# A recurrent attention layer with a sign-weight feed-forward gate: one load of the sums of squares, an earlier weight request, and two steps moved at a change of block

## The chip, the cores and the metric

The kernel runs on one core of a Trainium2 chip. A core has a matrix engine (TensorE, PE in the profile, with PEld for its weight loads), a vector engine (VectorE, DVE), a scalar engine (ScalarE, ACT), GpSimd (POOL) and SyncE (SP). SP issues most of the transfers between the large memory and the on-chip memory, and POOL issues those that add to what is already there. The matrix engine writes its results into result banks (PSUM), of which this kernel keeps six for its projections, and ScalarE or VectorE has to empty a bank before it can be used again.

The metric is device time in microseconds (us) for one execution; less is better.

## What is computed

The input x has 2048 tokens of 512 numbers. After a layer norm over the 512 numbers, the attention part runs 16 heads of 128 channels (2048 channels in all), and a feed-forward part of 2048 hidden units makes a gate. Inputs and outputs are float32. Cut to what matters:

```
xn = layernorm(x)
q, k, v = conv(silu(xn @ Wq)), conv(silu(xn @ Wk)), conv(silu(xn @ Wv))   # causal, 4 taps per channel
q, k = rotate(q), rotate(k);  q, k = q / |q|, k / |k|                      # per head and token
out = sum over s in 0..3 of  (q . lag(k, s)) / sqrt(128) * sigmoid(lag(a, s) * b) * lag(v, s)
out = out * rsqrt(mean(out^2) + eps) * norm_w * z                          # mean over all 2048 channels
s   = out @ Wout
g   = silu(relu(xn @ sign(up) * up_scale) @ sign(down) * down_scale * output_scale)
result = x + s * g
```

(The gate z is silu(xn @ Wz); a and b are xn @ Wa and xn @ Wb, one number per head and token.) The dots q . lag(k, s) need only four lags, so no token looks further back than three. The mean of out^2 needs all channels of a token. The kernel leaves this factor out of the output projection and applies it at the very end, when s is combined with g; for that it collects the sums of out^2, called o's sums below.

## The kernel before

**Tiling.** Channels lie on the 128 partitions and tokens along them. The tokens are cut into 4 blocks of 512 (index b), the heads into 8 pairs (index p, 256 channels each). The unit of work is `step(p, b)` (line 557). It makes q and k of pair p for block b + 1 and multiplies them (`queries`, `products`), and in the same step it makes v, the weighted sum o, the gate z and, every second pair, the output projection for pair p of block b. So attention runs one block behind the dots. The steps of block -1 (line 675) make only q and k, with the first quarter of the feed-forward part between them. Blocks 0 to 2 follow (line 695). A last stage (lines 699 to 761) does v, o, z and the projections of block 3, and a closing part (line 763 on) does the feed-forward part for blocks 1 to 3 and combines all.

**What happens when a block changes.** In the step with p = 0 and b >= 0 (`change` in line 560), all of block b's dots and squares of q and k are known, and the weights of v are made from them:

- `sum_squares` (line 390) adds the squares of q and k over channels, on TensorE; `sum_dots` (line 401) does so with the products for one pair or two.
- `norms(b)` (line 425) takes these squares through a copy and a square root on ScalarE and an addition and a maximum on VectorE.
- `norms_in_rows(b)` (line 438) takes the reciprocal on VectorE and then sends it to the rows rk and rq with eight transfers on SP.
- `coefficients(b)` (line 452) multiplies the rows with the gates and the dots in three VectorE instructions and writes the coefficients to memory (`co_dram`). `weighted` (line 483) later loads them back, spread over the channels, as bc ("coefficient rows"), in four transfers per pair; bc has three buffers.

For b = 1 and 2 the norms stand between q's and k's work (lines 564 to 568). For b = 0, and only there, they follow `products` (lines 569 to 571).

**Output projections** are collected in `outputs_due` and run by `output_projections` (line 550). One of them (line 528) covers two pairs and runs over four chunks of 128 tokens. After the last pair of a block `sums_of_o` (line 409) follows: TensorE adds o's squares over channels, POOL writes two rows of 512 sums into `ss_dram`, the second adding to the first, and SP loads them into `ss_acc`, one number per token with tokens on partitions (line 418).

**The order of work.** TensorE and VectorE execute in the order of the source: every instruction of theirs is pinned behind the one before it (`InOrder`, line 68; all show as line 76 in the profile). The instructions of ScalarE, SP and POOL are ordered by a planner. It issues what its own model of time takes as ready, the earlier in the source first, so a request for weights can be issued long ahead of its place in the source when its buffer is free. Within each engine's queue the order is then fixed. Buffers are shared by tag: the weights of v and z share three (`load`, line 246), rk and others share one.

**The last stage.** For block 3, line 700 on requests the weights of v for pairs 0 and 1, and the loop at line 730 requests those of pair p + 1 in round p, for p from 1 to 6. POOL loads the feed-forward part's signs for the up product in that loop (line 748). At its end line 759 takes a square root of all of `ss_acc` on ScalarE into `rms`, and VectorE the reciprocal. In the closing part POOL loads the signs for the down product (line 768), and hidden units go through `hid` (ScalarE, line 627), two casts on VectorE (`hid_hi`, `hid_lo`) and the down products.

Of the kernel before, what the change touches and what calls it, by code (L numbers as in the profile page):

```python
# [44 lines left out]
P = 128  # L45
# [8 lines left out]
NP = H // 2  # L54
TB = 512
NTB = S // TB
TC = TB // P
# [24 lines left out]
def recurrent_layer(ctx: ExitStack, tc: tile.TileContext, a: dict, out: bass.AP):  # L82
    nc = tc.nc
# [215 lines left out]
    outputs_due = []  # L299
# [24 lines left out]
    def products(p, b, q, between=None, beside_k=None):  # L324

        n = f"_{p}_{b}"
        load(qks, "k", p, b)
        q0 = q[:, LAGS - 1]
        k = with_halo(qks, "k", "k", 1, p, b)
        raw = raw_of(qks, "k", p, b)  # L330
        if p % 2 == 0:
            sum_squares()
        convolve(1, p, raw, k[:, :, HALO:])
        keep_halo("k", k, p, b)
        if between:
            between()
        turn(q)
        if beside_k:
            beside_k()

        sq = [qks.tile([P, 2, TB], F32, tag=f"sq{j}", name=f"sq{j}" + n, bufs=2 - j) for j in range(2)]
        for j in range(2):
            nc.scalar.activation(sq[j][:, 0], q0[:, j], AF.Square)
            nc.scalar.activation(sq[j][:, 1], k[:, j, HALO:], AF.Square)
        nc.gpsimd.dma_start(sq[0], sq[1], accum_op=ALU.add)
        squares_due.append((p, sq[0]))
        def product(to, j, lo, hi):

            k0 = k[:, j, lo : lo + TB]
            k_lags = bass.AP(k0.tensor, k0.offset, [k0.ap[0], [1, hi - lo], k0.ap[1]])  # L350
            dve.tensor_tensor(to, q[:, lo:hi, j, :], k_lags, ALU.mult)

        pr = qks.tile([P, LAGS, TB], F32, tag="pr", name="pr0" + n, bufs=2)
        product(pr, 0, 0, LAGS)
        if not b or p % 2 == 0:
            pr1 = qks.tile([P, LAGS, TB], F32, tag="pr", name="pr1" + n, bufs=2)
            product(pr1, 1, 0, LAGS)
            if b:
                nc.gpsimd.dma_start(pr, pr1, accum_op=ALU.add)
            else:  # L360
                dve.tensor_tensor(pr, pr, pr1, ALU.add)
        else:
            for lo in range(0, LAGS, 2):
                half = qks.tile([P, 2, TB], F32, tag="half", name=f"half{lo}" + n, bufs=1)
                product(half, 1, lo, lo + 2)
                dve.tensor_tensor(pr[:, lo : lo + 2], pr[:, lo : lo + 2], half, ALU.add)
        if not b:
            dots_due.append([p, pr, of_head[:, p], p == NP - 1, True])
            return


        for h in range(0, P, D // 2):
            first, second = slice(h, h + D // 4), slice(h + D // 4, h + D // 2)
            if p % 2 == 0:
                nc.gpsimd.dma_start(pr[first], pr[second], accum_op=ALU.add)
            else:
                both = dots_due[-1][1]
                nc.gpsimd.dma_start(both[second], pr[first])
                nc.gpsimd.dma_start(both[second], pr[second], accum_op=ALU.add)
        if p % 2 == 0:  # L380
            dots_due.append([p, pr, of_heads[:, p // 2], p == NP - 2, False])
        else:
            dots_due[-1][-1] = True
# [25 lines left out]
    def sums_of_o(b):  # L409

        so = mm.tile([P, TB], F32, tag="mm", name=f"so{b}")
        for j in range(2):
            add(so, j, ones, squares[b][:, j], True, True)
        row = vs.tile([P, HID], F32, tag="part", name=f"so_sb{b}", bufs=3)
        nc.scalar.copy(row[0 : 2 * LW], so[0 : 2 * LW])  # L415
        nc.gpsimd.dma_start(ss_dram[b : b + 1], row[0:1])
        nc.gpsimd.dma_start(ss_dram[b : b + 1], row[LW : LW + 1], accum_op=ALU.add)
        nc.sync.dma_start(
            ss_acc[:, b * TC : (b + 1) * TC], ss_dram[b].rearrange("(c p) -> p c", p=P)
        )  # L420

    squares = {}
    rows = {}
# [90 lines left out]
    def gated_output(p, b, o, z, wo):  # L514

        oz = vs.tile([P, 2, TB], F32, tag="oz", name=f"oz_{p}_{b}", bufs=3)
        for j in range(2):
            dve.scalar_tensor_tensor(
                oz[:, j, :], o[:, j, :], norm_w[:, p, j : j + 1], z[:, j, :], ALU.mult, ALU.mult
            )  # L520
        gated[p] = oz, wo
        if p % 2 == 1:
            pairs = gated.pop(p - 1), gated.pop(p)
            outputs_due.append(lambda: output_projection(p, b, *pairs))
        if p == NP - 1:
            outputs_due.append(lambda: sums_of_o(b))

    def output_projection(p, b, *pairs):

        for c in range(TC):  # L530
            po = mm.tile([P, HID], F32, tag="mm", name=f"po{c}_{p}_{b}")
            for i, (of, w) in enumerate(pairs):
                for j in range(2):
                    pe.matmul(
                        po,
                        of[:, j, c * P : (c + 1) * P],
                        w[:, j, :],
                        start=(i == 0 and j == 0),
                        stop=(i == 1 and j == 1),
                    )  # L540
            part = vs.tile([P, HID], F32, tag="part", name=f"part{c}_{p}_{b}", bufs=3)
            nc.scalar.copy(part, po)  # L542
            t = b * TC + c
            rows = s_dram[t * P : (t + 1) * P, :]
            if p == 1:
                nc.gpsimd.dma_start(rows, part)
            else:
                nc.gpsimd.dma_start(rows, part, accum_op=ALU.add)

    def output_projections():  # L550
        while outputs_due:
            outputs_due.pop(0)()


    first_due = []
# [1 line left out]
    def step(p, b, beside_q=None, beside_k=None):  # L557

        at = b >= 0
        change = p == 0 and at  # L560
        q = queries(p, b + 1)
        if beside_q:
            beside_q()
        if change and b:
            sum_squares()
            norms(b)
        due = bool(dots_due) and dots_due[0][-1]
        products(p, b + 1, q, (lambda: norms_in_rows(b)) if change and b else None, beside_k)
        if change and not b:
            norms(b)  # L570
            norms_in_rows(b)
        if p == NP - 1 and b + 2 < NTB:
            gate_products(b + 2)
        if at:
            load(vs, "v", p, b)
            raw = raw_of(vs, "v", p, b, 1)
        if due:
            sum_dots()
        if first_due:
            first_due.pop()()  # L580
        if at:
            v = values(p, b, raw)
        if change:
            coefficients(b)
        output_projections()
        if at:
            z, wo = gates_of_output(p, b)
            out_of = lambda: gated_output(p, b, weighted(p, b, v), z, wo)
            if change:
                first_due.append(out_of)  # L590
            else:
                out_of()
        if p == 1 and at:
            gate(b + 1)
        if b + 2 < NTB:
            if p < TC:
                statistics(b + 2, p)
            if p == TC - 1:
                centre(b + 2)
            elif p == 5:  # L600
                divide(b + 2)
# [128 lines left out]
    for p in range(NP + 1):  # L730
        if 1 < p < NP:
            raw = raw_of(vs, "v", p, last, 1)
        if p:
            z, wo = gates_of_output(p - 1, last, zs)
        if p % 2 == 1:
            output_projections()
        if p < NP - 1 and p:
            load(vs, "v", p + 1, last)
        if 0 < p < NP:
            zs = weights_of_output(p, last)  # L740
            v = values(p, last, raw)
        if p:
            gated_output(p - 1, last, o, z, wo)
        if p < NP:
            o = weighted(p, last, v)
        if p < NFC // G:
            some = slice(G * p, G * p + G)
            nc.gpsimd.dma_start(up[:, some], signs_dram["up"][:, some])
        elif p == NFC // G:
            nc.gpsimd.dma_start(first_down, signs_dram["down"][:, 0:NFD])  # L750
        if p == 4:
            xs = in_two_terms(ffw, tokens(1), "xs", 1, [P, KC, TB], "xs1")
# [3 lines left out]
    output_projections()  # L756
    nc.sync.dma_start(down_scale, a["down_scale"].partition_broadcast(P))
    nc.sync.dma_start(out_scale, a["out_scale"].partition_broadcast(P))
    nc.scalar.activation(rms, ss_acc, AF.Sqrt, bias=eps_rms, scale=1.0 / CH)
    dve.reciprocal(rms, rms)  # L760
    att.close()
# [161 lines left out]
```

## Time and profile before

| | |
|---|---|
| time, median of 3 runs | 1448.3 us (1445.02 to 1448.48) |
| profiled execution, own time | 1452.26 us |
| its span, first to last instruction | 1450.5 us |
| TensorE busy | 1404.1 us, 97% |
| VectorE busy | 1212.3 us, 84% |
| ScalarE busy | 612.6 us, 42% |
| GpSimd busy | 228.8 us, 16% |
| moved by DMA | 259.20 MB, mean 179 GB/s |
| matmuls v, out, q, z, k (512 records each) | 225 to 229 us each |

The profile is of one execution. Lines of a timeline give the start in us from the start of the span, the duration in us, the engine, the line, the operation with out<-in and the shape, and how many instructions are merged in the line. In square brackets stands how long the engine was idle before, and what released it. Where a wait is for several things, it is put down to the one that came last by the profile, which can be the wrong one. A line with SPq or POOL and DMA_DIRECT2D is the issue of a transfer; the data move later. TensorE's float32 matmuls show as two records each, at a distance of 0.43 us.

### The profile page before, as it was taken

What the parts mean: (1) busy time and instruction counts of PE and PEld (TensorE: products, weight loads), DVE (VectorE), ACT (ScalarE), POOL (GpSimd) and SP (SyncE); (2) the same over time, 40 slices, a digit from 0 to 9 for tenths busy, and PEclk for the clock granted to TensorE, in tenths of its full rate; (3) what the DMA queues carried; (4) which work ended last, traced back from release to release, by engine and by line L of the source; (5) the groups of instructions that cost most, each with busy time, mean ns of one, the idle gap of its engine ahead of it and who ended that gap; (6) DMA issues with size and microseconds to landing.
All of it is one profiled execution on the core that took longest, in us unless ns stands there. A gap on an engine that the chain in (4) does not pass through costs nothing.

```text
span 1450.5 us, 12563 instructions
## 1 busy us (share of the span) xinstructions
PE 1404.1 (97%) x3936; PEld 685.7 (47%) x3936; DVE 1212.3 (84%) x1363; ACT 612.6 (42%) x1181; POOL 228.8 (16%) x313
## 2 busy tenths in 40 slices
PE   7999999799999999999999999999996899999997
PEld 4555544244434444444444444444442344488886
DVE  6999997999999979999999899999893897246454
ACT  6575555345444443544444535444332333232122
POOL 2222110021212220112121202121211101200000
PEclk9999999999999999999999999999998899999999
DMA  9869577887999688779996798796769876562120
GB/s 339 258 162 223 139 196 159 207 202 170 201 206 203 139 179 226 198 185 192 209 200 156 165 227 209 172 218 155 160 136 258 206 192 150 83 226 92 35 88 29
DMA packets 101249, 259.20 MB, mean 179 GB/s; under 512 B 18816, under 2 KB 19328, under 8 KB 96320
## 3 DMA queue, kind: packets, MB, share of 16 engines
q0 software_dynamic: 32512, 104.89, 37.8%
q1 hardware_dynamic: 68672, 153.53, 36.5%
q8 instruction: 31, 0.51, 0.1%
q14 instruction: 34, 0.28, 0.1%
HBM read 157.67 MB, written 35.68 MB: 133 GB/s over the span
## 4 chain that ended last, share of the span: by engine, by line
PE 63%; DVE 26%; DMA 5%; issue 3%; ACT 2%; POOL 1%; SPq 0%; DVEq 0%; POOLq 0%; ACTq 0%
PE po L76 13%; PE pz L76 11%; PE pv L76 10%; PE pq L76 8%; DVE q L76 7%; PE pk L76 7%; PE ph L76 6%; PE pf L76 6%; DVE pr L76 5%; DVE k L76 4%; DMA pr<-pr 3%; DVE o L76 2%; DVE te L76 2%; DVE v L76 2%; DMA wv<-in_wv_dram 1%
## 5 line engine op out<-in xcount | busy, mean ns | idle before, releaser
L76 PE MATMUL pv<-xnT,wv 128*128 128x512 f32 x512 | 228.3, 598 | 17.6 <-DMA wv<-in_wv_dram 17.6
L76 PE MATMUL po<-wo,oz 128*128 128x512 f32 x512 | 227.8, 602 | 4.7 <-DVE oz L76 4.7
L76 PE MATMUL pq<-xnT,wq 128*128 128x512 f32 x512 | 228.7, 599 | 0.7 <-ACT xnT L173 0.7
L76 PE MATMUL pz<-xnT,wz 128*128 128x512 f32 x512 | 225.4, 592 | 0.0
L76 PE MATMUL pk<-xnT,wk 128*128 128x512 f32 x512 | 225.2, 592 | 0.0
L76 PEld LDWEIGHTS pv<-xnT,wv 128*128 128x128 f32 x512 | 96.4, 190 | 146.8 <-issue 137.2
L76 DVE SCALAR_TENSOR_TENSOR q<-rq,conv_w,q 128x512 f32<-128x512 f32 x192 | 141.4, 749 | 24.6 <-ACT q L284 20.0
L76 PEld LDWEIGHTS po<-wo,oz 128*128 128x128 f32 x512 | 97.2, 192 | 135.3 <-issue 111.0
L76 DVE SCALAR_TENSOR_TENSOR k<-rk,conv_w,k 128x512 f32<-128x512 f32 x192 | 142.1, 751 | 20.5 <-ACT k L284 15.8
L76 PEld LDWEIGHTS pq<-xnT,wq 128*128 128x128 f32 x512 | 97.1, 191 | 128.2 <-issue 119.5
L76 PEld LDWEIGHTS pz<-xnT,wz 128*128 128x128 f32 x512 | 96.4, 189 | 124.5 <-issue 120.7
L76 PEld LDWEIGHTS pk<-xnT,wk 128*128 128x128 f32 x512 | 96.6, 189 | 121.0 <-issue 116.4
L76 DVE SCALAR_TENSOR_TENSOR v<-rv,conv_w,v 128x512 f32<-128x512 f32 x192 | 141.3, 749 | 14.8 <-ACT v L284 10.3
L76 DVE SCALAR_TENSOR_TENSOR q<-q,turns 128x1024 f32<-128x1024 f32 (+1 forms) x128 | 127.1, 1013 | 2.3
L76 DVE TENSOR_TENSOR o<-o,te 128x1024 f32<-128x1024 f32 x96 | 117.6, 1225 | 3.3
L76 DVE TENSOR_TENSOR te<-v,bc 128x1024 f32<-128x1024 f32 x96 | 117.0, 1219 | 3.9 <-DMA bc<-co_dram 3.9
L76 DVE TENSOR_TENSOR pr<-q,k 128x2048 f32<-128x2048 f32 x52 | 117.4, 2289 | 1.0
L627 ACT ACTIVATE hid<-ph,up_scale 128x512 f32<-128x512 f32 x64 | 43.8, 684 | 121.0 <-PE ph L76 120.4
L76 DVE CAST hid_hi<-hid 128x512 fp32r<-128x512 f32 x64 | 27.1, 424 | 72.9 <-ACT hid L627 72.9
L76 PE MATMUL ph<-xs_hi,up 128*128 128x512 f32 x192 | 76.4, 398 | 0.7 <-ACT so_sb L415 0.7
L76 PE MATMUL ph<-xs_lo,up 128*128 128x512 f32 x192 | 75.8, 395 | 0.0
L542 ACT COPY part<-po 128x512 f32<-128x512 f32 x64 | 36.9, 579 | 88.4 <-PE po L76 53.5
(139 smaller groups left out, 1653.3 us busy)
## 6 DMA issues: line engine op xcount, KB each, us to landing
bc<-co_dram SPq DMA_DIRECT2D x128, 256.0 KB, 6.5
pr<-pr POOLq DMA_DIRECT2D x72, 256.0 KB, 6.1
wq<-in_wq_dram SPq DMA_DIRECT2D x32, 512.0 KB, 6.7
wk<-in_wk_dram SPq DMA_DIRECT2D x32, 512.0 KB, 7.0
sq<-sq POOLq DMA_DIRECT2D x32, 512.0 KB, 5.7
wv<-in_wv_dram SPq DMA_DIRECT2D x32, 512.0 KB, 4.9
wz<-in_wz_dram SPq DMA_DIRECT2D x32, 512.0 KB, 6.2
wo<-in_wo_dram SPq DMA_DIRECT2D x32, 512.0 KB, 6.5
```

Of the source, the lines that this page charges most:

```text
L76: return self.tc.keep_in_program_order(getattr(self.engine, op)(*args, **kwargs))
L542: nc.scalar.copy(part, po)
L627: nc.scalar.activation(hid, ph, AF.Relu, scale=up_scale[:, f : f + 1])
```

## The change

There are four edits.

1. **o's sums.** The load of `ss_acc` at the end of each `sums_of_o` (512 numbers, 4 bytes each, four times) is removed. One load of all 2048 stands ahead of the square root at the end of the last stage.
2. **Last dots between halves of an output projection.** At a change of block, `sum_dots` for the last pair is no longer ahead of `values`. `output_projections` now comes before `coefficients` and takes `sum_dots` as `midway`: the first projection that is due calls it after two of its four chunks. If nothing is due, it is called at once. The last stage still calls `sum_dots` and `output_projections` as before.
3. **v's weights.** In the last stage, the weights of v for pair 2 are requested in round 0, ahead of `weighted` (the coefficient rows of pair 0), in place of round 1. The other requests keep their rounds.
4. **Norms behind q's turns.** At the change with b = 0, `norms` and `norms_in_rows` are passed to `products` as `beside_k`, which it calls after `turn(q)` and ahead of the squares and the products.

```diff
@@ sums_of_o @@
         nc.gpsimd.dma_start(ss_dram[b : b + 1], row[0:1])
         nc.gpsimd.dma_start(ss_dram[b : b + 1], row[LW : LW + 1], accum_op=ALU.add)
-        nc.sync.dma_start(
-            ss_acc[:, b * TC : (b + 1) * TC], ss_dram[b].rearrange("(c p) -> p c", p=P)
-        )
@@ gated_output, output_projection @@
-            outputs_due.append(lambda: output_projection(p, b, *pairs))
+            outputs_due.append(lambda midway: output_projection(p, b, midway, *pairs))
         if p == NP - 1:
-            outputs_due.append(lambda: sums_of_o(b))
+            outputs_due.append(lambda midway: sums_of_o(b))
 
-    def output_projection(p, b, *pairs):
+    def output_projection(p, b, midway, *pairs):
 
         for c in range(TC):
+            if midway and c == TC // 2:
+                midway()
@@ output_projections @@
-    def output_projections():
+    def output_projections(midway=None):
+        if midway and not outputs_due:
+            midway()
         while outputs_due:
-            outputs_due.pop(0)()
+            outputs_due.pop(0)(midway)
+            midway = None
@@ step @@
+        if change and not b:
+
+            def beside_k():
+                norms(b)
+                norms_in_rows(b)
+
         products(p, b + 1, q, (lambda: norms_in_rows(b)) if change and b else None, beside_k)
-        if change and not b:
-            norms(b)
-            norms_in_rows(b)
...
-        if due:
+        if due and not change:
             sum_dots()
         if first_due:
             first_due.pop()()
         if at:
             v = values(p, b, raw)
+
+        output_projections(sum_dots if change else None)
         if change:
             coefficients(b)
-        output_projections()
@@ last stage @@
-        if p < NP - 1 and p:
-            load(vs, "v", p + 1, last)
+        if p < NP - 1 and p != 1:
+            load(vs, "v", max(p + 1, 2), last)
...
+    nc.sync.dma_start(ss_acc, ss_dram.rearrange("b (c p) -> p (b c)", p=P))
     nc.scalar.activation(rms, ss_acc, AF.Sqrt, bias=eps_rms, scale=1.0 / CH)
     dve.reciprocal(rms, rms)
```

## The prediction

> **What bounds the kernel now.** I read the page's first part, then what TensorE waited for, then the timelines around each wait. The first part says that TensorE is nearly the whole span: 1450.5 - 1404.1 leaves 46 us idle, of which some 15 are start and tail.
>
> ```profile
> span 1450.5 us, 12563 instructions
> PE 1404.1 (97%) x3936; PEld 685.7 (47%) x3936; DVE 1212.3 (84%) x1363; ACT 612.6 (42%) x1181; POOL 228.8 (16%) x313
> ```
>
> The view of waits, TensorE alone (total us, times, longest), names nearly all the rest. Only what shortens these waits, or makes a new one, moves the end.
>
> ```profile
> PE pv L76 <- DMA wv<-in_wv_dram: 17.6, 1, 17.6
> ...
> PE po L76 <- DVE oz L76: 4.7, 3, 3.8
> PE dots L76 <- DVE v L76: 4.4, 1, 4.4
> PE dots L76 <- DMA pr<-pr: 3.2, 1, 3.2
> ```
>
> By the timeline of TensorE the 4.4 and the 3.8 stand together, at 276 to 290 us. I call this place A; the 17.6 (1111.7 to 1129.3) is place C.
>
> ```profile
> 280.59 1.94 PE L76 MATMUL dots<-pr,of_heads 128*32 128x512 f32 x8 [4.44 <-DVE v L76]
> 282.45 3.78 PE L76 MATMUL po<-wo,oz 128*128 128x512 f32 x4
> 290.01 10.52 PE L76 MATMUL po<-wo,oz 128*128 128x512 f32 x20 [3.78 <-DVE oz L76]
> ```
>
> **Edit 1, norms behind q's turns (the first change of block): -4.6 us.** The start of place A is in VectorE's timeline some 50 us earlier. VectorE waits there for rows that it made late itself:
>
> ```profile
> 221.48 4.49 DVE L76 TENSOR_TENSOR pr<-q,k 128x2048 f32<-128x2048 f32 x2
> 225.89 0.67 DVE L76 TENSOR_TENSOR r<-sq,squares 64x512 f32<-64x512 f32 x1
> ...
> 228.18 3.35 DVE L76 RECIPROCAL r<-r 64x512 f32<-64x512 f32 x1 [1.09 <-ACT r L435]
> 231.45 4.46 DVE L76 SCALAR_TENSOR_TENSOR v<-rv,conv_w,v 128x512 f32<-128x512 f32 x6
> 240.36 0.69 DVE L76 TENSOR_TENSOR rq<-rq,gate 128x512 f32<-128x512 f32 x1 [4.45 <-DMA rq<-r]
> 243.97 0.69 DVE L76 SCALAR_TENSOR_TENSOR rk<-dots,rk 128x512 f32<-128x512 f32 x1 [2.92 <-DMA gate<-ab_dram]
> ```
>
> The reciprocal lets SP issue eight row transfers, the first at 231.55 and the last at 236.44; the chain that ended last gives the last one 7.21 us, so it lands at 243.65. That is 12.1 us after the first issue, and it, not the gate transfer named, releases 243.97.
>
> In the new order norms stand ahead of the two products. Their inputs are there: ScalarE has copied the squares by 217.9, q's turns end at 221.45. Add 0.67, max 0.49, wait for ScalarE's square root (1.09 now; the table load of 1.28 may be bare, so up to 2.2), reciprocal 3.35: done at 227.15 against 231.5. Rows land 12.1 later, at 239.3. Products and v's convolution (4.41 + 4.55) now stand behind the reciprocal and end at 236.2, so VectorE again waits for rows, and takes the dots at 239.4 for 243.97: 4.6 us sooner. From the bottom: if ScalarE puts z's evictions of 223.48 ahead of the square root, 2.4 remain; from the top: all 7.37 us of waiting gone. I take 4.6, since the eight rows are the same.
>
> From 245.3 on VectorE runs without a gap to oz at 290, so oz comes at 285.4. TensorE reaches this projection by 282 and still waits there, so the 4.6 arrive in full. The pr additions on POOL's queue for pair 0 start 5.6 us later (226.28 becomes about 232), but their user is POOL's next addition at 266.6, hence hidden. From 290 to 1111 TensorE waits 3.3, 0.7, 0.8 and 0.2 us only; these move with it.
>
> **Edit 2, dots between halves of the output projection (next two changes): 0.** TensorE issues the same matmuls. Half a projection is 16 records of 0.43, so the dots end about 7 us later: near 515.3 and 803.7. VectorE reads them at 526.82 and 819.06, kept back by its own convolutions: 11 and 15 us of cover. Were it gone, the 7 us would go to coefficients and then to oz, which TensorE already awaits at 583.2 (0.67). The projection starts 1 us sooner; its oz has stood since 500.1 and 792.3. At the first change nothing is due, and in the last stage no half is passed.
>
> **Edit 3, v's weights: 0.** It moves one call, the third weight of the last block (pair 2). SP's timeline shows requests out of source order, as buffers come free:
>
> ```profile
> 1066.97 0.33 SPq L248 DMA_DIRECT2D wv<-in_wv_dram  x1
> ...
> 1098.29 2.61 SPq L493 DMA_DIRECT2D bc<-co_dram  x4
> 1108.22 0.37 SPq L418 DMA_DIRECT2D ss_acc<-ss_dram  x1
> 1108.64 3.01 SPq L493 DMA_DIRECT2D bc<-co_dram  x4
> 1111.69 0.59 SPq L248 DMA_DIRECT2D wv<-in_wv_dram  x1
> ```
>
> Counting back from the last of 32 requests, pair 2's is the one at 1066.97: already 31 us ahead of the coefficient rows. The late one at 1111.69, which TensorE awaits, is pair 3's, and its call stays behind pair 1's rows. Bounds: 0, and up to -10.5 if SP's order changes (rival 2).
>
> **Edit 4, o's sums loaded once: three loads away, 0; one at the end, +10.6.** SP stood at the removed loads from 537.7 to 542.25, 830.1 to 834.21 and 1100.9 to 1108.22. Behind them were coefficient rows. In the first two cases VectorE is at work until 559 and 847 and takes the rows without a wait. In the third, two of the four rows behind need a buffer that VectorE frees at 1110.4, so pair 3's request still leaves at about 1111. The single DMA packets say the same of the queue: SP's queue moves pair 0's rows until 1114.3, then the load's 512 packets of 4 bytes until 1119.5, against packets of 8 KB from POOL's up load. It went packet by packet:
>
> ```
> us        POOL's queue, 8 KB   SP's queue
> 1103      40                   40 of 2 KB
> 1115      49                   50 of 4 B
> 1116      50                   57 of 4 B
> 1118      50                   50 of 4 B
> ```
>
> Without the 4-byte packets, the 257 remaining 8 KB packets share with 2 KB rows at 32 of each per us (8.0 us), then 255 rows at 105 per us (2.4): pair 3's weights start at 1124.7, against 1124.4 now. Place C stays.
>
> At the end all four loads become one, 2048 packets of 4 bytes. Behind it stand ScalarE's square root (rms) and VectorE's reciprocal, and behind those, in fixed order, the casts of hid 2, which TensorE needs for its third down product at 1276.80. Four timelines, one line each:
>
> ```profile
> 1273.26 0.38 SPq L418 DMA_DIRECT2D ss_acc<-ss_dram  x1
> 1273.86 1.69 POOL L768 DMA_DIRECT2D down<-down_signs  x3 [1.87 <-DMA ss_dram<-so_sb]
> 1275.41 0.31 ACT L759 ACTIVATE rms<-ss_acc,eps_rms 128x16 f32<-128x16 f32 x1 [0.17 <-DMA ss_acc<-ss_dram]
> 1275.76 0.25 DVE L76 RECIPROCAL rms<-rms 128x16 f32<-128x16 f32 x1 [21.93 <-ACT rms L759]
> ```
>
> Now the casts start at 1275.92, under 1 us of slack. The packets of today's load run from 1274.25 to 1274.95, up to 208 in 0.25 us. POOL's down load, 384 packets of 8 KB, starts moving at 1275.7. Until then some 1170 of 2048 pass; the other 880 go one to one with down, 50 per us: 384/50 = 7.7 us, to 1283.4; the last 490 take 0.6. Landing 0.4 later is 1284.4, for 1275.4: rms 1284.7, casts from 1284.95, TensorE at 1285.4. The wait is 8.6 us, and after such gaps TensorE starts slowly: 20 records from 290.01 took 10.52 for 8.6, 16 from 1129.35 took 8.95 for 6.87. So 2.0 more: +10.6. No work covers it; the down products that follow are TensorE's own.
>
> Here the Trainium skill speaks twice the other way. "DMA: Bandwidth & Descriptors", section "Anatomy of one DMA — SWDGE (gpsimd) path", prices a transfer (there on GpSimd's path) at some 2.0 us fixed plus its bytes over 436 GB/s: 8 KB would land as 2 KB did (2.2 us by the trace), the sum being -4.6. Its section "Queues, rings and completion order" lets an engine drain 9 to 17 descriptors from one ring before it turns to the next: 880/16 = 55 per engine would be about 5 turns of 0.33 us, an estimate of a landing near 1278 and a wait near 2, the sum -2.6. The trace shows turns of one packet at 1115 to 1119, in the same kind of load against the same kind of neighbour. I take the row.
>
> **Sum.** -4.6 + 0 + 0 + 10.6 = +6.0 on the span: 1456.5, and 1458.3 for the profiled execution (1452.26 now). That execution is 4 us above the median of the runs, so on the median: 1448.3 + 6.0 = 1454.3.
>
> **Rivals.**
> 1. The last load slips through before down: wait 2, no slow start, sum -2.6, **1445.7**. For it: over half its packets go before down moves. Against: the row above. Chance 0.14.
> 2. Faster: SP's order changes with ss_acc gone, and pair 3's weights go ahead of pair 1's rows, at the end of their buffer's use (1097.8) or soon after. TensorE would go on at 1111.7, but by 1118.6 lack result banks until ScalarE empties pair 2's at about 1125: gain at most 19.6 - 7 - 2 = 10.5, sum -4.5, **1443.8**. It decides once the landing moves by over 6 us, to before 1123. For it: SP's order does follow readiness. Against: nothing in the source puts this call ahead. Chance 0.17.
> 3. The norms stall VectorE mid-stream, or POOL's delayed additions come late: edit 1 gives 0, **1459**. For it: VectorE is 97% busy from 250 to 300. Against: the old order waited no less. Chance 0.16.
> 4. Edits 1 and 4 cancel, or neither does anything: **1448**. Chance 0.03.
>
> The forecast keeps 0.50; its own range, from 2.4 to 7.3 for edit 1 and 9 to 12 for the end, is 1450 to 1458.
>
> **Chances.** 0.3% is 4.3 us, about what a measurement can tell from no change. Slower (over 1452.6): 0.46 from the forecast and rival 3 whole, 0.62. Faster: 0.15 from rival 2 and 0.03 from rival 1 where edit 1 gives its top, 0.18. Within: 0.04 of the forecast, 0.11 of rival 1, 0.02 of rival 2 and rival 4 whole, 0.20. Range 1444 to 1461: below it rivals 1 and 2 together, above it rival 3 with a further stall.
>
> **What would show it.** VectorE takes the dots near 239 in the first change (edit 1); TensorE's wait for oz near 286 shrinks or the earlier one for dots goes. The 17.6 us wait for wv stays. The ss_acc load needs about 11 us to land, and TensorE waits 8 to 9 us for hid 2's casts at about 1272 to 1281. If the load lands within 5 us, edit 4's step is wrong; if pair 3's wait shrinks by over 3 us, edit 3's is.

## The result, and the profile after

Edits are numbered here as in the prediction: edit 1 moves the norms, edit 4 loads o's sums once. The list under "The change" has these two the other way round.

| | before | changed |
|---|---|---|
| median of 22 runs each, taken side by side | 1448.53 us (1445.02 to 1457.59) | 1446.03 us (1439.57 to 1456.16) |
| changed / before, 95% interval | | 0.9978 [0.9965, 0.9992] |
| profiled execution, own time | 1452.26 us | 1442.18 us |
| its span | 1450.5 us | 1440.4 us |

The ratio makes 3.2 us of 1448.5 (1.2 to 5.1): a small gain, where the forecast was a loss of 6. Its size is below the 0.3% that a measurement of this kernel can tell; the interval leaves out "no change", but narrowly. The two profiled executions differ by 10.1 us, three times as much as the medians, so most of this section asks what of the 10.1 belongs to the change.

The first part of the page of the changed kernel:

```profile
span 1440.4 us, 12555 instructions
PE 1401.4 (97%) x3936; PEld 685.1 (48%) x3936; DVE 1211.9 (84%) x1363; ACT 612.9 (43%) x1181; POOL 228.8 (16%) x313
```

TensorE executes the same 3936 matmul records, and its busy time fell by only 2.7 us (1404.1 to 1401.4; records last longer after a wait, as told below, and there are fewer waits). The other 7.4 of the 10.1 are idle time. The view of TensorE's waits of the changed kernel (total us, times, longest):

```profile
PE pv L76 <- DMA wv<-in_wv_dram: 15.7, 1, 15.7
...
PE po L76 <- DVE oz L76: 6.2, 3, 5.3
PE dots L76 <- issue: 0.8, 1, 0.8
...
PE pf L76 <- DVE hid_hi L76: 0.3, 1, 0.3
PE pf L76 <- DVE hid_lo L76: 0.2, 1, 0.2
```

Beside the list of before: the wait of 4.4 us for VectorE at the dots of place A is gone, and so is the one of 3.2 us for `pr`. The wait for wv (place C) is 1.9 shorter. The wait for oz has grown from 3.8 to 5.3. And at the end, where 8.6 us for the casts were forecast, stand 0.3 and 0.2.

To see which of these belong to which edit, cut TensorE's time into four stretches at three marks: its resume at place A (the first `po` after the wait for oz), its first sum of o of block 2 (`so`, just ahead of place C), and the first up product after its last sum of o (just ahead of the new load). Eleven profiles, in us; each mark is a start in TensorE's timeline:

| kernel | start to A | A to `so` of block 2 | on to the first up product after the last `so` | on to the end | span |
|---|---|---|---|---|---|
| before | 290.0 | 799.9 | 177.5 | 183.15 | 1450.5 |
| before, second execution | 289.9 | 797.4 | 175.8 | 183.12 | 1446.2 |
| changed | 284.6 | 796.5 | 175.5 | 183.80 | 1440.4 |
| changed, second execution | 285.3 | 798.3 | 179.2 | 183.75 | 1446.6 |
| changed, third execution | 283.0 | 799.0 | 176.1 | 183.68 | 1441.8 |
| norms alone (edit 1) | 283.3 | 795.2 | 176.2 | 183.13 | 1437.8 |
| one load alone (edit 4) | 289.6 | 796.3 | 179.5 | 183.90 | 1449.3 |
| dots between halves alone (edit 2) | 290.3 | 806.6 | 173.7 | 183.48 | 1454.1 |
| changed without edit 1 | 290.0 | 801.0 | 178.4 | 184.27 | 1453.7 |
| changed without edit 4 | 284.5 | 801.8 | 176.1 | 183.24 | 1445.6 |
| changed, end load three times | 284.1 | 803.6 | 177.3 | 196.99 | 1462.0 |

(The twelfth profile, with POOL's loads held back, is told below.) The first and the last stretch follow the edits: the first takes 289.6 to 290.3 without edit 1 and 283.0 to 285.3 with it; the last takes 183.1 to 183.5 without the load at the end and 183.7 to 184.3 with it. The two between vary by up to 11 and 6 us in no clear order of edits, and by 2.5 and 3.7 among three executions of the changed kernel itself. So the change is worth about -5.6 in the first stretch and +0.6 in the last, and most of what else separates two single profiles is not the change's.

What the middle stretches vary by can be read off. The profile gives the TensorE clock that was granted (the column PEclk), and in and behind a long wait it is 0.5 for some microseconds. In the changed kernel at place A:

```profile
core 0: us, PE busy (x) PEld busy (x) DVE busy (x) ACT busy (x) POOL busy (x), PEclk, DMA share, GB/s
282.60:289.40 6.80, 4.76 (x6) 2.18 (x7) 6.59 (x10) 5.14 (x8) 0.95 (x2) 0.50 1.06 213
289.40:300.00 10.60, 10.60 (x26) 4.59 (x26) 10.28 (x14) 4.86 (x12) 2.54 (x4) 1.00 0.63 160
```

At 0.5 TensorE starts a record every 0.85 us, at 1.00 every 0.43. This is the slow start of the prediction. Take from the second stretch its waits (0.9 to 8.2 us) and half of TensorE's busy time at 0.5 (busy for 3.4 to 10.2 us): in all twelve profiles 792.3 to 793.7 is left. The third leaves 157.3 to 157.5. So nothing but waits, and the clock behind them, moves these two stretches by more than 1.4 us. Over the whole execution TensorE was busy at 0.5 for 12.7 us before and for 8.4 in the changed kernel, which makes 2.2 of the 2.7 us of busy time above.

Where the gain is made is in VectorE's timeline of the changed kernel (the same instructions as those shown of before):

```profile
218.91 4.06 DVE L76 SCALAR_TENSOR_TENSOR q<-q,turns 128x512 f32<-128x512 f32 x4 [1.75 <-ACT q L312]
222.89 0.67 DVE L76 TENSOR_TENSOR r<-sq,squares 64x512 f32<-64x512 f32 x1
...
225.93 3.35 DVE L76 RECIPROCAL r<-r 64x512 f32<-64x512 f32 x1 [1.92 <-ACT r L432]
229.21 4.42 DVE L76 TENSOR_TENSOR pr<-q,k 128x2048 f32<-128x2048 f32 x2
233.55 4.55 DVE L76 SCALAR_TENSOR_TENSOR v<-rv,conv_w,v 128x512 f32<-128x512 f32 x6
238.01 0.69 DVE L76 TENSOR_TENSOR rq<-rq,gate 128x512 f32<-128x512 f32 x1
238.62 0.69 DVE L76 SCALAR_TENSOR_TENSOR rk<-dots,rk 128x512 f32<-128x512 f32 x1
```

The products and v's convolution stand behind the reciprocal and fill the flight of the rows. The lines at 238.01 and 238.62 have no bracket: nothing is waited for, where 4.45 and 2.92 us stood before. The dots are taken at 238.62 for 243.97, 5.35 us sooner.

At the end, four timelines (SP, POOL, ScalarE, VectorE), one line each:

```profile
1262.47 0.38 SPq L765 DMA_DIRECT2D ss_acc<-ss_dram  x1
1263.07 1.70 POOL L775 DMA_DIRECT2D down<-down_signs  x3 [1.87 <-PE ph L76]
1265.62 0.31 ACT L766 ACTIVATE rms<-ss_acc,eps_rms 128x16 f32<-128x16 f32 x1 [1.12 <-DMA ss_acc<-ss_dram]
1265.96 0.25 DVE L76 RECIPROCAL rms<-rms 128x16 f32<-128x16 f32 x1 [22.89 <-ACT rms L766]
```

From the issue to the square root it is 3.1 us. The load of a quarter of the size took 2.2 before, and 11 had been forecast. The single DMA packets of the two kernels show why (packets that start in each stretch):

```
before, 512 packets of 4 B, per 0.25 us from 1274.25:    133  208  180
changed, 2048 packets of 4 B, per 0.25 us from 1263.75:  239  344  412  457  423

changed, us      SP's queue, 4 B   POOL's queue, 8 KB
1263             313               -
1264             1636              2
1265             115               38
1266             -                 49
```

The 208 per 0.25 us that the forecast took for the queue's pace were only its first half microsecond. A longer load goes on to over 400, and all 2048 are through when down's packets begin in earnest. It repeats: in the six profiles of kernels with this one load, 1442 to 1913 of the packets are through before down's first, where the forecast had 1170, and the rest follow within 0.6 us.

### The profile page after: what moved, and what is told of

Its sections match the earlier page's. It is cut to its first block, busy times and chain, and to the rows that moved or that the text cites. A ratio compares the mean times of both kernels' runs of the same rounds, so it can differ in the third digit from the quotient of the medians.

```text
span 1440.4 us, 12555 instructions
## 1 busy us (share of the span) xinstructions
PE 1401.4 (97%) x3936; PEld 685.1 (48%) x3936; DVE 1211.9 (84%) x1363; ACT 612.9 (43%) x1181; POOL 228.8 (16%) x313
## 4 chain that ended last, share of the span: by engine, by line
PE 65%; DVE 21%; issue 6%; DMA 4%; ACT 2%; SPq 1%; POOL 0%; DVEq 0%; POOLq 0%; ACTq 0%
PE po L76 11%; PE pq L76 10%; PE pz L76 10%; PE pk L76 9%; PE pv L76 8%; PE ph L76 7%; PE pf L76 7%; DVE q L76 4%; DVE o L76 3%; DVE v L76 3%; DVE te L76 3%; DVE k L76 2%; DVE pr L76 2%; DMA wv<-in_wv_dram 1%; DVE oz L76 1%
## 5 line engine op out<-in xcount | busy, mean ns | idle before, releaser
L76 PE MATMUL pv<-xnT,wv 128*128 128x512 f32 x512 | 228.2, 598 | 15.7 <-DMA wv<-in_wv_dram 15.7
L76 DVE SCALAR_TENSOR_TENSOR v<-rv,conv_w,v 128x512 f32<-128x512 f32 x192 | 141.4, 750 | 11.7 <-ACT v L284 7.2
L272 ACT ACTIVATE rq<-pq 128x512 f32<-128x512 f32 x64 | 38.1, 596 | 83.5 <-PE pq L76 83.3
```

The source lines that it names most:

```text
L76: return self.tc.keep_in_program_order(getattr(self.engine, op)(*args, **kwargs))
L272: nc.scalar.activation(to[:, j, :], pp, AF.Silu)
```

## The experiments

Medians are over all runs of a kernel that were taken beside the kernel before; ratios are against the kernel before, with 95% intervals. An expectation names two theories; its letters are explained in it.

### Edit 1 alone: the norms behind q's turns

```diff
-        products(p, b + 1, q, (lambda: norms_in_rows(b)) if change and b else None, beside_k)
         if change and not b:
-            norms(b)
-            norms_in_rows(b)
+
+            def beside_k():
+                norms(b)
+                norms_in_rows(b)
+
+        products(p, b + 1, q, (lambda: norms_in_rows(b)) if change and b else None, beside_k)
```

> Only the norms of the first change are moved; all else is the kernel before. Theory T (the gain is edit 1's, the end load costs next to nothing): 3 to 5 us faster than before, VectorE takes the dots of the first change near 239 instead of 244, and the wait of TensorE at 276 to 290 falls from 8.2 to about 5. Rival R (the gain comes from SP's queue, freed of the three loads): 0, within 1 us.

Measured: 1446.03 us against 1450.99, ratio 0.9964 [0.9948, 0.9980], that is -5.2 us (-2.9 to -7.5). VectorE takes the dots at 237.24. TensorE's waits:

```profile
PE pv L76 <- DMA wv<-in_wv_dram: 16.7, 1, 16.7
...
PE po L76 <- DVE oz L76: 6.7, 3, 5.8
```

The wait for wv is there in full, and the wait for the dots at place A is gone. The gain of the whole change is found with this edit alone, as theory T had it (it gave 3 to 5 us).

### Edit 4 alone: one load of o's sums at the end

```diff
         nc.gpsimd.dma_start(ss_dram[b : b + 1], row[LW : LW + 1], accum_op=ALU.add)
-        nc.sync.dma_start(
-            ss_acc[:, b * TC : (b + 1) * TC], ss_dram[b].rearrange("(c p) -> p c", p=P)
-        )
...
     nc.sync.dma_start(out_scale, a["out_scale"].partition_broadcast(P))
+    nc.sync.dma_start(ss_acc, ss_dram.rearrange("b (c p) -> p (b c)", p=P))
```

> Only the loads of o's sums are changed. Theory T: within 1 us of before; TensorE waits about 0.5 us for the casts of hid 2, place C (the wait for wv) within 2 us of 17.6. Rival R: 2 to 4 us faster, by a shorter wait at place C. The forecast on record: 10.6 us slower.

Measured: 1453.99 us against 1450.99, ratio 1.0020 [1.0004, 1.0035]: +2.9 us (0.6 to 5.1). No gain, so rival R falls; but it is also more than the 1 us that theory T allowed. Its waits:

```profile
PE pv L76 <- DMA wv<-in_wv_dram: 18.8, 1, 18.8
...
PE dots L76 <- DVE v L76: 5.1, 1, 5.1
...
PE pf L76 <- DVE hid_hi L76: 0.3, 1, 0.3
```

Of the loss, the profile shows 0.75 us in the last stretch (183.90 for 183.15). Place C is no better with three loads fewer on SP's queue: 18.8 here, 17.6 and 15.1 in two executions of the kernel before. Whether it is worse, and holds the rest of the 2.9, is taken up below; the lower end of the interval needs no rest.

### The change without edit 1, and without edit 4

These are the changed kernel with the diffs above turned round. The first:

> The changed kernel with the norms of the first change back behind the products. Theory T: within 1 us of before, the wait at 276 to 290 is 8.2 again. Rival R: as fast as the changed kernel, 3 us under before.

Measured: 1451.9 us, ratio 1.0011 [0.9997, 1.0026], so 1.6 us over before with no change inside the interval. With the norms back in their old place nothing of the gain is left, and TensorE resumes at place A at 290.04. The second:

> The changed kernel with the four loads of o's sums back in their places. Theory T: 3 to 5 us faster than before, like the norms alone, perhaps 0.5 more than the changed kernel. Rival R: within 1 us of before.

Measured: 1447.16 us, ratio 0.9978 [0.9958, 0.9997], the same as the whole change. TensorE waits 15.4 us for wv, and not at all for the casts of hid. So edit 4's price in the runs is 0 by this pair and 2.9 by the pair before, each uncertain by 2 to 4 us, with 0.6 to 0.7 at the end in the profiles.

### Edit 2 alone: dots between the halves

The edit is the one in `output_projection`, `output_projections` and `step`; its core:

```diff
-        if due:
+        if due and not change:
             sum_dots()
...
+
+        output_projections(sum_dots if change else None)
         if change:
             coefficients(b)
-        output_projections()
```

> Only the last dots of two changes of block are moved between the halves of the output projection. Theory T: the same time as before, within 1 us; VectorE reads the dots at the same places, 11 to 15 us after TensorE has made them. Rival D (the later dots hold VectorE up, or oz is not ready for the earlier half): over 2 us slower, with a longer wait of TensorE for oz near 580 and 870.

Measured: 1449.38 us against 1448.08, ratio 0.9997 [0.9976, 1.0017]. Medians and ratio differ in sign; the edit does nothing that can be measured. In TensorE's timeline of the changed kernel the dots stand between two half projections (16 records each), and nothing waits for them:

```profile
505.54 1.06 PE L76 MATMUL dots<-pr,of_heads 128*32 128x512 f32 x8
506.53 7.13 PE L76 MATMUL po<-wo,oz 128*128 128x512 f32 x16
```

Edit 3 alone was not run, because there is nothing to run: with it and without it, the compiled program has the same instructions in the same order on every engine, against the kernel before and within the changed kernel. The planner had issued pair 2's request ahead of the coefficient rows already.

### Three times the load at the end

Was the forecast's mechanism wrong (turns of one packet each between the two queues), or only its pace? If the turns are real, a load long enough to be still under way when down moves must pay them. This kernel makes the load three times, the first two into tiles that nobody reads:

```diff
+    ss_again = ffw.tile([P, NT], F32, name="ss_again")
+    ss_more = ffw.tile([P, NT], F32, name="ss_more")
...
-    nc.sync.dma_start(ss_acc, ss_dram.rearrange("b (c p) -> p (b c)", p=P))
+    for to in (ss_again, ss_more, ss_acc):
+        nc.sync.dma_start(to, ss_dram.rearrange("b (c p) -> p (b c)", p=P))
```

> The changed kernel, with the 2048 numbers loaded three times at the end, the last time into the tile that is used, so 6144 packets of 4 bytes stand ahead of rms. In the changed kernel 2048 packets passed in 1.8 us, before the down load moved. Theory K (the forecast was right on the turns of one packet, wrong only on the rate): the first 2048 pass as before, the other 4096 meet the down load; 384 go one to one with its 384 packets in some 7.7 us, the rest in 2 us, so TensorE waits 9 to 12 us for the casts of hid 2 and the kernel is 9 to 13 us slower than the changed one. Rival L (small packets are not held up by large ones): 4096 more at 1800 per us are 2.3 us, a wait of about 3 us, and 3 us slower than the changed kernel.

Measured: 1459.53 us, ratio 1.0081 [1.0053, 1.0109], where the changed kernel has 0.9978: 13 to 15 us more (between the medians, or by the ratios), a little over the 9 to 13 of theory K. The last stretch takes 196.99 us for 183.80. TensorE's waits, and then the load and its square root by their lines (ns min/median/max, first and last start):

```profile
PE pf L76 <- DVE hid_hi L76: 11.8, 2, 11.1
```

```profile
L768 SPq DMA_DIRECT2D ss_acc<-ss_dram x1: 6834/6834/6834, 1272.7 to 1272.7; - x1
L769 ACT ACTIVATE rms<-ss_acc,eps_rms x1: 307/307/307, 1284.8 to 1284.8; 128x16 f32<-128x16 f32 x1
```

TensorE waits 11.1 us for the casts of hid 2: the very wait that was forecast, behind the very chain. The packets, per us:

```
us        POOL's queue, 8 KB   SP's queue, 4 B
1272      -                    1193
1273      16                   871
1274      37                   -
1275      52                   10
1276      46                   241
1277      53                   60
1278      51                   53
1279      50                   64
1280      49                   49
1281      30                   701
1282      -                    2594
```

The first load's packets are through in two microseconds. From 1277 to 1280 the rest runs beside down nearly one packet for one, 49 to 64 per us for 49 to 53. Before that it is not so regular: for two microseconds SP's queue moves next to nothing, then 241 packets in one. In all 789 of the 4096 pass before down's last packet, where theory K had 384, and the others follow at up to 2594 per us. The second load had been issued by 1272.64, so that SP was held up with the third does not explain it. Theory L falls and K holds in the main: a small packet waits while down moves, about one to each of down's, and the changed kernel escapes because its load is over in time. (The records give no engine for a packet, so the turns are read from counts over all 16.)

### POOL's loads for the feed-forward part held back

Place C is the largest wait before and after, and no edit moves it. In the changed kernel POOL issues five loads of 1 MB (four of `up`, one of `first_down`) within 4.2 us, about when SP starts on the rows and the weights that the kernel's last stage needs:

```profile
1088.36 0.59 POOL L754 DMA_DIRECT2D up<-up_signs  x1 [3.75 <-DMA co_dram<-rk]
1090.05 1.94 POOL L754 DMA_DIRECT2D up<-up_signs  x3
1091.69 0.82 POOL L756 DMA_DIRECT2D first_down<-down_signs  x1
```

The source spreads them over rounds; the planner draws them together. This kernel keeps them in the order of the source on POOL's queue, and one round later, so that each stands behind the squares of one pair:

```diff
-        if p < NFC // G:
-            some = slice(G * p, G * p + G)
-            nc.gpsimd.dma_start(up[:, some], signs_dram["up"][:, some])
-        elif p == NFC // G:
-            nc.gpsimd.dma_start(first_down, signs_dram["down"][:, 0:NFD])
+        if 0 < p <= NFC // G:
+            some = slice(G * p - G, G * p)
+            tc.keep_in_program_order(nc.gpsimd.dma_start(up[:, some], signs_dram["up"][:, some]))
+        elif p == NFC // G + 1:
+            tc.keep_in_program_order(nc.gpsimd.dma_start(first_down, signs_dram["down"][:, 0:NFD]))
```

> The changed kernel, with POOL's five loads of 1 MB in the last stage (up signs and first down) held in source order behind the squares of o of pairs 1 to 5, in place of all five at once at the start. Every other queue is the same. Theory V (place C is made by the volume of these 5 MB on the shared DMA engines, not by where SP requests wv): the wait for wv falls from 15.7 to under 4 us and the kernel is 12 to 17 us faster than the changed one. Rival O (SP's order is what makes wv late): the wait stays above 10 us and the time within 3 us of the changed kernel.

Measured: 1435.31 us (1432.33 to 1439.67) against 1448.08, ratio 0.9903 [0.9872, 0.9935], that is -14.0 us (-9.4 to -18.5) on the kernel before. The changed kernel's whole interval lies above this one: the pacing itself is worth some 0.75%, 11 us, a little under the 12 to 17 of theory V. It is the fastest kernel of this study. The view of TensorE's waits:

```profile
PE po L76 <- DVE oz L76: 9.8, 4, 6.3
...
PE dots L76 <- DMA ss<-o: 3.6, 1, 3.6
...
PE pv L76 <- ACT ss L504: 1.3, 1, 1.3
```

The wait for wv has gone from the list, and 1.3 us for ScalarE stand where it was. Place C in TensorE's timelines, of the changed kernel:

```profile
1095.96 7.03 PE L76 MATMUL pz<-xnT,wz 128*128 128x512 f32 x16
1118.66 8.89 PE L76 MATMUL pv<-xnT,wv 128*128 128x512 f32 x16 [15.67 <-DMA wv<-in_wv_dram]
```

and of this one:

```profile
1104.57 7.03 PE L76 MATMUL pz<-xnT,wz 128*128 128x512 f32 x16
1112.91 7.11 PE L76 MATMUL pv<-xnT,wv 128*128 128x512 f32 x16 [1.32 <-ACT ss L504]
...
1131.24 13.97 PE L76 MATMUL po<-wo,oz 128*128 128x512 f32 x28 [2.63 <-DVE oz L76]
```

The third stretch of the table above (from `so` of block 2 to the first up product) takes 163.9 us here, and 175.5 to 179.2 in the changed kernel. By its parts: 14.4 of waiting less, 1.8 of slow start less (7.11 for 8.89), and given back 2.6 at the projection that follows, where oz is now the last to come. The slow start behind that wait takes another 1.9, so 11.7 is left, and 11.6 less is found against the fastest of the three. The second stretch was long in this execution (805.2), which hides most of the gain in its own span of 1437.9; it was the slowest of this kernel's six runs. So place C is made by what POOL's loads move at that time, theory V, and not by the order of SP's queue, which is the same in both. Two lines of SP's timeline show how, in the changed kernel:

```profile
1087.80 15.55 SPq L490 DMA_DIRECT2D bc<-co_dram  x8
1103.40 0.59 SPq L248 DMA_DIRECT2D wv<-in_wv_dram  x1
```

and here:

```profile
1098.07 8.87 SPq L490 DMA_DIRECT2D bc<-co_dram  x8
1106.98 0.59 SPq L248 DMA_DIRECT2D wv<-in_wv_dram  x1
```

Beside POOL's loads the eight coefficient rows take SP 6.7 us longer to issue. The packets show the sharing again: in the changed kernel 64 packets of 2 KB from SP's queue pass in 2 us (1102 to 1104) beside 63 of 8 KB from POOL's, and in this kernel 228, with no 8-KB packet beside them. Then wv itself takes 15.3 us from its request to TensorE's start (1103.40 to 1118.66), for 5.9 here (1106.98 to 1112.91).

### Further executions of the same kernels

Is the spread of the second stretch a property of a kernel's queues, or of an execution? The changed kernel and the kernel before, profiled again as they are:

> The changed kernel, unchanged, profiled in a second execution. The stretch from TensorE's resume at place A to its first sum of o of block 2 took 796.5 us in the first profile of this kernel, 799.9 in that of the kernel before, and 795 to 807 in the other kernels, with no order by edits. Theory S (it differs from execution to execution, since TensorE's waits for dots near 431 and 720 us come and go): this look gives another value than 796.5 by 2 us or more, anywhere from 794 to 808, with waits for dots to match. Rival F (each kernel has its fixed value, set by the order of its queues): within 1 us of 796.5 and no wait for dots above 1 us. Both: TensorE resumes at place A at 283 to 285.5, and from the first up product after the last sum of o to the end it takes 183.6 to 184.3 us.

> The changed kernel in a third execution. Theory S: of the three profiles of this kernel at least two differ by 2 us or more in the stretch from place A to the first sum of o of block 2, and the time of the execution follows. Rival F: all three within 1 us of 796.5.

> The kernel before, unchanged, in a second execution. Theory S: the stretch from place A to the first sum of o of block 2 may lie anywhere from 794 to 808 (799.9 in the first profile). Rival F: within 1 us of 799.9, with a wait for dots of about 3.2 us near 431. Both: TensorE resumes at place A at 289.5 to 290.5, and the end takes 183.0 to 183.5 us from the first up product after the last sum of o.

The second stretch took 798.3 and 799.0 in the changed kernel (796.5 at first) and 797.4 in the kernel before (799.9 at first). The third execution differs from the first by 2.5 us, and the second by 1.85, a little under the 2 that theory S asked for; rival F, which allowed 1, falls. In the first profile of before TensorE waited 3.2 us for dots near 431 us. In the second it does not, and waits 2.5 us near 721 instead. TensorE's waits of that second execution:

```profile
PE pv L76 <- DMA wv<-in_wv_dram: 15.1, 1, 15.1
PE dots L76 <- issue: 8.6, 2, 6.2
...
PE po L76 <- DVE oz L76: 3.5, 3, 2.7
```

(The 6.2 is the wait at place A, under another name than in the first profile; with the 2.7 for oz behind it, it makes 8.9, where the first profile had 4.4 and 3.8.) At the marks of edit 1 and edit 4 the executions repeat within 0.1 us for before (289.9, and 183.12) and within 2.3 and 0.1 for the changed kernel (283.0 to 285.3, and 183.68 to 183.80); 283.0 is at the edge of what was expected.

## Why the prediction was wrong, point by point

**What bounds the kernel: right.** What moved is TensorE's waits in the list and the slow start behind them, to within 2 us in each stretch.

**Edit 1, forecast -4.6: right in its main path, and close partly by luck.** Place A moved by -5.4 in the first pair of profiles, by -5.6 in the means of two and three executions (289.95, 284.31), and the runs give -5.2 with the edit alone. Two of the inner steps were off, against each other. The reciprocal was to end at 227.15 and ended at 229.28: q's turns waited 1.75 us for ScalarE, because the planner put the copy of the squares ahead of q's part there, and the wait for the square root was 1.92, inside the range given. The rows were to land 12.1 us after their first issue and so to be the last; the trace has the last at 236.01, 6.7 us after it (229.31). The forecast had carried over 7.21 us from the last issue to the landing; here it took 2.11 (233.90 to 236.01). The packets suggest why. Before, 8-KB packets of POOL's `pr` additions, issued at 226.28 and 235.16, share the DMA engines with the rows, and for two microseconds (237 to 239) no row moves. With the products behind the reciprocal the first addition is issued at 233.92, and its packets begin at 235, when the rows are nearly through. The prediction named this delay but counted it only as hidden. So VectorE's own work ended last, at 238.01, and no wait for rows was left. That oz comes the same amount sooner, and that TensorE still waits for it, was right: 283.83 for 289.20, and 5.3 us of waiting, longer than before because the wait for the dots ahead of it is gone. Some of the gain is given back behind the mark: TensorE is busy at the clock of 0.5 for 4.6 us of the second stretch (mean of three executions) for 3.4 before, which costs 0.6.

**Edit 2, forecast 0: right.** 0.9997 alone, and the dots have users late enough.

**Edit 3, forecast 0: right.** The order of every queue is the same. Rival 2 needed SP's order to change and falls with that.

**Edit 4, the three loads away, forecast 0: no gain, as forecast; a small loss stays open.** The wait at place C is 15.1 and 17.6 before, and 13.7 to 16.7 in three other kernels that keep the three loads. In six executions without them it is 15.7, 16.2, 17.6, 17.8, 18.5 and 18.8. The means are 15.7 with the loads and 17.4 without. That would make up the rest of edit 4's 2.9, but with spreads of 3 to 4 us in so few executions it is not shown.

**Edit 4, the load at the end, forecast +10.6: here the prediction failed.** The step is the pace in "until then some 1170 of 2048 pass". It was read from the 512-packet load, at most 208 in 0.25 us, and held constant; that load is over while it is still gathering pace. The longer load reached 457 in 0.25 us, so instead of 880 packets left for the turns with down there were some 140 to 600, which passed while down was starting. In place of a wait of 8.6 and a slow start of 2.0 the profiles show waits of 0.3 and 0.2 and a last stretch 0.6 to 0.7 longer. (Down's first packets before are at 1275.17, not 1275.7; by the forecast's own rule this leaves its sum as it is.) The step behind it, turns of about one packet at 50 per us, was right in the main, as the threefold load shows: the price is there when much of the load is left once down is in full flow, and the changed kernel stays just short of that. The two passages of the Trainium skill that were weighed against the row ("DMA: Bandwidth & Descriptors", sections "Queues, rings and completion order" and "Anatomy of one DMA — SWDGE (gpsimd) path") gave sums nearer to what came, but not by their rules: the packet counts of the threefold load, 49 to 64 for 49 to 53, are those of turns of about one packet, not of 9 to 17, and the load took 3.1 us for 2.2, where bytes alone would have made no difference.

**The sum.** With 0.7 for the last term it is -4.6 + 0 + 0 + 0.7 = -3.9, and with the measured place A, less the 0.6 given back, -5.6 + 0.6 + 0.6 = -4.4; the runs have -3.2 (-1.2 to -5.1). Rival 1, the load that slips through, is what happened: it had 1445.7, and the median is 1446.03. That the two are so close is partly luck, since it gave the end 2.0 us and edit 1 4.6. It was given 0.14 on the strength of one row of packets that was too short to show the pace.

**What stays open.** Why the waits for dots near 431 and 720 us come and go between executions of one kernel, at up to 3.8 us each, and whether edit 4 costs more in the median than the 0.6 to 0.7 us that the profiles show at the end, perhaps at place C.

## What to carry to other kernels

A rate read from a short transfer is the rate of its start. Before a longer one is priced with it, ask whether the counts were still rising when it ended, and give the price both ways: here the whole sign hung on it. A transfer of small packets that competes with one of large packets pays once both are in full flow, so the question is which one is through first. And a wait for weights may be made neither by the place of their request nor by the order of their queue, but by what another queue started 12 to 15 us earlier: five loads of 1 MB that nobody needed for over 140 us (TensorE's first up product in the last stage is at 1236.9) cost this kernel 11 us, and holding them back is a change of a few lines. Last, one profile of each kernel is not enough for a change of 0.2%: take TensorE's waits and the time lost at the lower clock out first, and compare what is left.

## What was not expected of the hardware

- Loads of single 4-byte elements gather pace: 133 to 208 packets per 0.25 us in a load of 512, up to 457 in one of 2048 and 2594 per us in the queue left alone behind down. Four times the packets took 1.4 times as long from issue to use (3.1 us for 2.2).
- Between SP's small packets and POOL's 8-KB packets the sharing comes near one to one in number, not in bytes: 49 to 64 of 4 B for 49 to 53 per us in the threefold load (1277 to 1280), 64 of 2 KB for 63 in 2 us at place C. The record of a 4-byte packet lasts 9 ns when alone and 43 to 203 ns (mean of each us) beside down, and its queue falls from 2594 to some 50 packets per us.
- In and behind a wait of 5.3 us TensorE's granted clock was 0.5 (282.6 to 289.4 in the changed kernel), and records came every 0.85 us for 0.43.
- SP itself can be held: with two loads of 2048 packets issued just ahead, issuing the third took 6.83 us, where the only one of the changed kernel took 0.38.
- The same program, with the same order on every engine, had its waits for dots at different places in different executions, and its second stretch moved by 2.5 us. One profile of each of two kernels would have put the change at -10.1 us; the runs have -3.2.
